# Normalised, padded frames kept in DRAM: written once in the statistics pass, read again by the 5x5 convolution and by the last layer, which multiplies straight out of PSUM

## The chip, the cores and the metric

The kernel runs on one core of one Trainium2 chip. The metric is the device time of one launch in microseconds (us): the median of the runs shown.

## The reference, cut to what matters

The input x is 16 images of 32 channels of 128x128, in float32. Four layers follow, each of the form x + f(gn(x)), where gn normalises groups of two channels. Layer 0 is a recurrent (LSTM) sweep over diagonals. Layer 1 is an adder layer: minus the sum of |patch - w| over 3x3 taps and 32 channels, on quantised values. Layer 2 mixes 32x32 modes of a Hartley transform. Layer 3, which the change touches, is this:

```
orig = x                                  # here x is gn(x3), x3 the result of layer 2
y = conv3x3(get_operator(x), conv1)       # five normalised edge operators, then a 3x3 conv
y = maxpool2(y); y = conv3x3(y, conv2); ... ; y = deconv2x2(y, deconv3)
y = conv3x3(y, conv7)
return orig * y                           # and the layer returns x3 + orig * y
```

So the result is x3 + gn(x3) * y. The edge operators and the first 3x3 convolution are folded into one 5x5 convolution, whose weights depend on means and variances of the operators' outputs over each image.

## The kernel before

**Stages.** `stage0` does layer 0. `rest` does everything else. In it, `Differences.run` does layer 1: for each of 16 images and 2 halves it makes 72 difference tiles of 128 x 8192 float16 values, some on VectorE (line 708), the others on ScalarE (line 705), and TensorE sums each (line 595). Which engine makes the next one is decided while the program is written, by whichever is planned to be done first.

**Layers 2 and 3 are background work.** `After.work` is a Python generator that handles images in four groups of four. Group g can start when image 4g + 3 has left layer 1. Its steps are `forward` (transform), `encoder` and `last`. `encoder` runs `back` (the inverse transform, which writes x3 to DRAM), `first_layers` (`statistics`, the weight tables, `conv1`, conv2) and `small_layers`. A partition holds one channel of one of the group's four images.

**The order is written out by a planner.** `Weave` holds planned clocks for TensorE, VectorE and ScalarE (`weave.pe`, `weave.dve`, `weave.act`). A background step that yields a positive number takes so many planned us of TensorE; a negative one is a pause; `later(us, step)` puts a step off; `("done", v)` has a put-off step carried out and waits for its planned end. Background TensorE work is put between the sums of layer 1 as long as the sums are not planned to be more than 3 us late (`SLACK`). `keep_busy` (line 625) fills holes in TensorE with matmuls by zero weights. `keep_order` then fixes each engine's queue in just this order; all large DMAs are on SyncE's queue (SP) and are issued in that order too, each behind the waits of those before it. Groups 0 to 2 are woven into layer 1. When layer 1 is done, `drain` alternates between what is left of them (the "left" chain) and group 3 (the "right" chain).

**Frames.** `frames` (line 1283 on) holds a ring of tiles `xp` of [128, 20, 132]: 16 rows of x3, two more above and below, and a border of two columns. The left chain has two such tiles, the right four. `load` (line 1307) brings half a tile from x3, rows of 512 bytes; `normalise` (lines 1309 to 1323) scales and shifts it on ScalarE (1313), zeroes the outermost row on GpSimd (1316), and copies the reflected row (1317) and columns (1319, 1320). This is done for all 16 halves in `statistics` (Gram matmuls at line 1354, edge columns at 1384), and once more for all 16 in `conv1` (matmuls at line 1671). A half is reloaded 2 us of plan after its last use.

**The last layer.** `last` (line 1735 on) loads x3 in four units of 32 rows into `xr` (line 1742), computes the composed deconv3 and conv7 into PSUM (lines 852 and 877), and for each of 8 rounds and 4 images does two VectorE instructions of 128x512:

```
s = acc * istd + (istd * bias + 1)        # line 1800, TENSOR_SCALAR, written interleaved
x = (x - mean) * s                        # line 1763, SCALAR_TENSOR_TENSOR
```

`done` then adds the mean on ScalarE (line 1773), and `store` writes a unit to the output in four DMAs of 4 KB rows (line 1779).

Of the kernel before, what the change touches and what calls it, by code (L numbers as in the profile page):

```python
# [16 lines left out]
HW = H * W  # L17
CHW = C * HW
NG = 4
M1 = 32  # L20
RND = 12582912.0


# [882 lines left out]
class After:  # L906
# [379 lines left out]
    def frames(self, g, pool):  # L1286

        nc, x3, weave = self.nc, self.d["x3"], self.weave
        ring = [pool.tile([128, 20, W + 4], F32, name=f"xp{i}") for i in range(self.buffers["frames"])]
        for t in ring:
            nc.vector.memset(t[:, :, 0], 0.0)
            nc.vector.memset(t[:, :, W + 3], 0.0)

        chunk = lambda ch: ring[ch % len(ring)]

        def parts(ch, half):

            lo, hi = max(16 * ch - 2 + 10 * half, 0), min(16 * ch + 8 + 10 * half, H)
            off = lo - (16 * ch - 2)
            return chunk(ch), lo, hi, chunk(ch)[:, off : off + hi - lo, 2 : W + 2]

        def load(ch, half):
            t, lo, hi, v = parts(ch, half)
            nc.sync.dma_start(v, bc_view(x3, g).rearrange("p (h w) -> p h w", w=W)[:, lo:hi, :])

        def normalise(ch, half, us):
            t, lo, hi, v = parts(ch, half)  # L1310

            def step():
                nc.scalar.activation(v, v, AF.Identity, bias=self.shift3, scale=self.stats3[:, 1])  # L1313
                for edge, r, src, zero in ((lo == 0, 1, 3, 0), (hi == H, 18, 16, 19)):
                    if edge:
                        nc.gpsimd.memset(t[:, zero, :], 0.0)
                        nc.scalar.copy(t[:, r, 2 : W + 2], t[:, src, 2 : W + 2])
                own = slice(10 * half, 10 * half + 10)
                nc.scalar.copy(t[:, own, 1], t[:, own, 3])  # L1319
                nc.scalar.copy(t[:, own, W + 2], t[:, own, W])  # L1320
                weave.act += 2.0

            return weave.later(us, step)

        return load, normalise, chunk

    def statistics(self, g, pool, frames, sides, out, tables):

# [4 lines left out]


        nc, cst, weave = self.nc, self.cst, self.weave
        load, normalise, chunk = frames
# [26 lines left out]
        for ch in range(H // 16):  # L1363
            xp = chunk(ch)
            yield ("done", ready[ch, 0])
            for l in range(2, 18):
                if l == 8:
                    yield ("done", ready[ch, 1])
                r = 16 * ch + l - 2
                own = [r2 for r2 in (r, r + 1) if (r, r2) in GRAM_AT]  # L1370
                if own:
# [21 lines left out]
                weave.dve += 0.3  # L1393

                def following(ch=ch, half=half):
                    load((ch + ahead) % 8, half)
                    if ch + ahead < H // 16:
                        ready[ch + ahead, half] = normalise(ch + ahead, half, 18.0)

                ready[ch + ahead, half] = weave.later(2.0, following)  # L1400
            yield -1.0
# [210 lines left out]
    def conv1(self, g, pool, frames, y1, sides, wf, b1):  # L1612
# [9 lines left out]
        load, normalise, chunk = frames  # L1622
        ahead = self.buffers["frames"]
        ready = {(n // 2, n % 2): normalise(n // 2, n % 2, 4.0 + 3.0 * n) for n in range(2 * ahead)}
        p = self.acc()
        for j in range(4):
            nc.tensor.matmul(p[32 * j : 32 * j + 32, :4], tap_of("all", 25), cst["m4_bc"], start=True, stop=True)
# [30 lines left out]
        spreads = []  # L1658
        for ch in range(H // R):
            xp = chunk(ch)  # L1660
            yield ("done", ready[ch, 0])
            yield ("done", ready[ch, 1])

            acc = [self.acc() for _ in range(4)]
            edge = {0: ("t", 0, 0, 1), H // R - 1: ("b", 3, 3 * W, 17)}.get(ch)
# [32 lines left out]
            yield SUMMED  # L1698
            if ch + ahead < H // R:
                for half in range(2):  # L1700
                    load(ch + ahead, half)
                    ready[ch + ahead, half] = normalise(ch + ahead, half, 26.0 + 4.0 * half)
            out = []
            for blk in range(4):
                a4 = acc[blk].rearrange("p (r w) -> p r w", w=W)
# [21 lines left out]
    def last(self, g):  # L1727

        nc, tc, cst, weave = self.nc, self.tc, self.cst, self.weave
        with self.pool("l_y") as yp, self.pool("l_x", self.buffers["l_x"]) as xp:  # L1730
# [1 line left out]
            y6 = self.y6  # L1732
            up = self.up7.loaded(yp)

            def at(t, unit, j):
                first = t.offset + g * 4 * CHW + (32 * unit + 8 * j) * W
                return bass.AP(t.tensor, first, [[HW, 32], [CHW, 4], [1, 8 * W]])

            def load(unit):
                xr = xp.tile([128, 4, 8 * W], F32, name="xr3")  # L1740
                for j in range(4):
                    nc.sync.dma_start(xr[32 * j : 32 * j + 32], at(self.d["x3"], unit, j))
                return xr

            xr = [load(unit) for unit in range(ahead)]

# [7 lines left out]
            nc.vector.tensor_copy(ms, p[:, :8])  # L1754
            mean, istd = ms[:, 0:4], ms[:, 4:8]

            one = yp.tile([128, 4], F32, name="l_one")
            nc.vector.tensor_scalar(one, istd, up.bias, 1.0, ALU.mult, ALU.add)
            yield -4.0

            def multiply(x, s, pr, blk):
                v = x[:, blk].rearrange("p (r a w) -> p a r w", a=2, w=W)[:, pr]
                nc.vector.scalar_tensor_tensor(
                    v, v, mean[:, blk : blk + 1], s.rearrange("p r w b -> p r (w b)"), ALU.subtract, ALU.mult
                )
                weave.dve += 0.7


            following = {}

            def done(x, unit):
                for blk in range(4):
                    nc.scalar.activation(x[:, blk], x[:, blk], AF.Identity, bias=mean[:, blk : blk + 1])
# [16 lines left out]
            for unit in range(4):  # L1790
                complete(unit - ahead)
                x = xr[unit]
                for pr in range(2):
# [2 lines left out]
                        yield from up.round(y6, 64, acc, lambda j: (2 * pr + pc, 16 * unit + 4 * j, 4, 256 * pc))  # L1796
                    yield SUMMED
                    for blk in range(4):
                        s = yp.tile([128, 4, 64, 2], F32, name="s", bufs=3)
                        nc.vector.tensor_scalar(  # L1800
                            s.rearrange("p r w b -> p b r w"),
                            acc[blk].rearrange("p (b r w) -> p b r w", b=2, w=64),
                            istd[:, blk : blk + 1],
                            one[:, blk : blk + 1],
                            ALU.mult,
                            ALU.add,
                        )
# [134 lines left out]
def program(nc, tc, a, at, out):  # L1942
    def scratch(name, *shape):
        return nc.dram_tensor(name, shape, F32, kind="Internal").ap()
# [4 lines left out]
    d["y6"] = scratch("y6_d", NG, 128, 66 * 66)  # L1949
# [30 lines left out]
```

## Time and profile before

| what | value |
|---|---|
| median of 3 runs | 7199.5 us (7186.45 to 7207.52) |
| span of the profiled execution, first to last instruction | 7206.6 us |
| layer 0 | 0 to about 880 us |
| layer 1 with the background work of groups 0, 1 and a part of 2 | about 880 to 5942 us |
| what is left after layer 1 | 5942 to 7206.6 us |
| `conv1` of groups 0 and 1 | 2824 to 3330 us, 4450 to 4970 us |
| `last` of groups 0 and 1 | about 3530 to 3700 us, 5190 to 5355 us |
| group 2 at 5942 us | in `statistics`: about a quarter of its matmuls done |

No total is recorded for the profiled execution besides its span, which is 7.1 us above the median and inside the interval of the runs.

In the profile's rows, a line is a line of the kernel; "x" is a count; "busy" is the sum of durations; a row of the windows view gives, for a stretch of time, each engine's busy time with the number of its instructions, the TensorE clock granted as a share of full speed, the share of time for which the 16 DMA engines were busy, and GB/s. Rows of a timeline give start, duration, engine, line, operation, tiles and count; the idle time ahead of it and what ended it stand in brackets. Consecutive instructions of one engine overlap a little, so the distance of two starts, not the duration, is what an instruction takes from the engine.

### The profile page before, as it was taken

How to read it: one execution, taken by the hardware profiler on the slowest of the kernel's cores; microseconds unless marked ns; L12 is line 12 of the kernel's file. 1: busy time of each engine (PE TensorE's matmuls, PEld its weight loads, DVE VectorE, ACT ScalarE, POOL GpSimd, SP SyncE). 2: the span in 40 equal slices, each digit the busy share in tenths (PEclk: the TensorE clock that was granted, in tenths of full speed). 3: DMA queues.
4: the chain of work that ended last, by engine and by line, in shares of the span. 5: the costliest groups of instructions: out<-in, count | busy, mean ns of one | idle time of the engine just before them, and what ended most of it. 6: DMA issues, size and time to landing. Idle time of an engine off the chain costs nothing. (4 is left out here: it accounts for less than half of the span.)

```text
span 7206.6 us, 271424 instructions
## 1 busy us (share of the span) xinstructions
PE 5631.0 (78%) x127740; PEld 3001.3 (42%) x127740; DVE 5845.3 (81%) x7099; ACT 5498.0 (76%) x3100; POOL 111.8 (2%) x91
## 2 busy tenths in 40 slices
PE   4778567777877777998777787999776784797896
PEld 3665333333334343333334343333333443554564
DVE  7787689999998989999998999999998994134224
ACT  2555489999998989999999999999998991131222
POOL 0000000000000000000000001000000000000000
PEclk9899789999988898999888998999888986798997
DMA  8664211111133432221343343221252245252324
GB/s 310 230 205 144 83 63 57 55 58 47 47 101 93 141 98 81 63 69 47 78 126 98 115 118 104 65 65 46 57 134 92 64 136 150 89 170 74 86 51 98
DMA packets 372719, 722.57 MB, mean 100 GB/s; under 512 B 50896, under 2 KB 217296, under 8 KB 360720
## 3 DMA queue, kind: packets, MB, share of 16 engines
q1 hardware_dynamic: 364128, 670.79, 30.6%
q0 software_dynamic: 7040, 33.80, 1.4%
q8 instruction: 999, 16.37, 1.0%
q14 instruction: 120, 0.98, 0.0%
q10 hardware_dynamic: 432, 0.64, 0.0%
HBM read 507.28 MB, written 164.32 MB: 93 GB/s over the span
## 5 line engine op out<-in xcount | busy, mean ns | idle before, releaser
L705 ACT ACTIVATE d_act<-q,neg 128x8192 f16<-128x8192 f16 (+1 forms) x631 | 4462.6, 7143 | 184.4 <-PE acc L595 135.0
L708 DVE TENSOR_SCALAR d_dve<-q,qw 128x8192 f16<-128x8192 f16 (+1 forms) x1673 | 3859.4, 2362 | 200.8 <-PE acc L595 158.0
L595 PE MATMUL acc<-d_dve,sel 128*32 128x512 f16 x26768 | 1869.8, 402 | 504.0 <-DVE d_dve L708 454.0
L595 PEld LDWEIGHTS <-sel 128*32 128x32 f16 x36864 | 1026.9, 100 | 2164.4 <-issue 1507.8
L1671 PE MATMUL acc<-xp,wf 32*32 32x512 f32 x25600 | 1043.7, 618 | 37.6 <-issue 32.8
L595 PE MATMUL acc<-d_act,sel 128*32 128x512 f16 x10096 | 724.4, 408 | 356.2 <-ACT d_act L705 343.6
L1671 PEld LDWEIGHTS acc<-xp,wf 32*32 32x32 f32 x25600 | 431.9, 104 | 416.5 <-issue 329.6
L625 PE MATMUL acc<-q,zero 128*32 128x512 f16 x7248 | 522.9, 401 | 0.0
L1609 ACT ACTIVATE y<-pooled,b 32x128 f32<-32x128 f32 x488 | 195.0, 400 | 414.4 <-DVE pooled L1595 407.8
L207 PE MATMUL pg<-h,wb 64*64 64x20 f32 (+15 forms) x4096 | 395.7, 320 | 106.1 <-DVE h L256 64.8
L852 PE MATMUL acc<-y,u_conv 32*32 32x256 f32 (+1 forms) x9728 | 359.8, 459 | 76.0 <-issue 46.6
L244 ACT ACTIVATE gt<-pg,bias 128x20 f32<-128x20 f32 (+15 forms) x1024 | 315.8, 374 | 80.2 <-PE pg L207 73.1
L1313 ACT ACTIVATE xp<-xp,shift,stats 128x1280 f32<-128x1280 f32 (+1 forms) x128 | 182.6, 1434 | 240.5 <-DMA xp<-x_d 210.1
L207 PE MATMUL pg<-e,wb 64*64 64x20 f32 (+15 forms) x4096 | 353.1, 315 | 16.4 <-DVE e L260 5.4
L207 PEld LDWEIGHTS pg<-h,wb 64*64 64x64 f32 x4096 | 248.3, 154 | 140.7 <-DVE h L256 90.4
L625 PEld LDWEIGHTS <-zero 128*32 128x32 f16 x7248 | 218.6, 102 | 203.0 <-issue 46.1
L207 PE MATMUL pg<-xn,wb 64*64 64x28 f32 (+61 forms) x4096 | 284.5, 302 | 11.3 <-ACT gt L244 3.8
L207 PEld LDWEIGHTS pg<-e,wb 64*64 64x64 f32 x4096 | 251.5, 156 | 92.1 <-DVE e L260 62.9
L1354 PE MATMUL acc<-xp 32*64 32x204 f32 (+3 forms) x8576 | 238.5, 344 | 37.8 <-ACT xp L1319 28.8
L1800 DVE TENSOR_SCALAR s<-acc,l_ms,l_one 128x512 f32<-128x512 f32 x128 | 102.3, 824 | 199.0 <-PE acc L852 199.0
L255 ACT ACTIVATE th<-c 128x20 f32<-128x20 f32 (+15 forms) x256 | 81.3, 320 | 235.5 <-DVE c L253 234.1
L852 PEld LDWEIGHTS acc<-y,u_conv 32*32 32x32 f32 x9728 | 171.4, 110 | 196.6 <-issue 130.4
(215 smaller groups left out, 4303.1 us busy)
## 6 DMA issues: line engine op xcount, KB each, us to landing
xr<-x_d SPq DMA_DIRECT2D x192, 512.0 KB
xp<-x_d SPq DMA_DIRECT2D x112, 640.0 KB
q<-q_d SPq DMA_DIRECT2D x32, 2145.0 KB
x_d<-xr SPq DMA_DIRECT2D x128, 512.0 KB
x_in<-in_x_dram SPq DMA_DIRECT2D x16, 2048.0 KB
res<-in_x_dram SPq DMA_DIRECT2D x64, 512.0 KB
xn<-in_xs_dram SPq DMA_DIRECT2D x64, 512.0 KB
xn<-xn SPq DMA_DIRECT2D x128, 256.0 KB
```

The lines of the kernel that those rows point to most:

```text
L207: nc.tensor.matmul(bank[c][q][64 * pair : 64 * pair + 64, :, :width], wb[half, 4 * kind + KIND[q]].rearrange("p b o -> p (b o)"), v[half], ...
L244: nc.scalar.activation(gt[:, q, :, :n], bank[c][q][:, :, :n], AF.Tanh if q == G else AF.Sigmoid, bias=bias[:, KIND[q] : KIND[q] + 1],)
L595: self.nc.tensor.matmul(acc[k][32 * j : 32 * j + 32, :], self.sel16[:, i // 9, :], d[:, row : row + 4, c : c + W], start=first, stop=last,)
L625: self.nc.tensor.matmul(acc[k][32 * j : 32 * j + 32, :], self.zero, q[:, :4, :W], start=False, stop=False)
L705: nc.scalar.activation(dst, src, AF.Relu, bias=self.neg[:, i : i + 1])
L708: nc.vector.tensor_scalar(dst, src, self.qw[:, i : i + 1], 0.0, ALU.subtract, ALU.max)
L852: nc.tensor.matmul(acc[blk][32 * j : 32 * j + 32, o : o + rows * n], t[part, 4 * par + tap, :], src[part, top : top + rows, left : left + ...
L1313: nc.scalar.activation(v, v, AF.Identity, bias=self.shift3, scale=self.stats3[:, 1])
L1354: nc.tensor.matmul(gram[blk][j : j + width, at : at + n], xp[part, l, 2 + j : 2 + j + width], xp[part, rows, j : j + width + 4], start=sta ...
L1609: nc.scalar.activation(d, s, AF.Identity, bias=bj)
L1671: nc.tensor.matmul(acc[blk][32 * j : 32 * j + 32, :], tap_of("all", tap)[rows], xp[rows, 4 * j + kh : 4 * j + kh + 4, kw : kw + W], start= ...
L1800: nc.vector.tensor_scalar(s.rearrange("p r w b -> p b r w"), acc[blk].rearrange("p (b r w) -> p b r w", b=2, w=64), istd[:, blk : blk + 1] ...
```

## The change

1. A DRAM tensor `xn` holds every padded, normalised frame: 128 x 132 x 132 values for each group. (An unused tensor, `y6`, goes.)
2. In `statistics`, each half of a frame is stored to `xn` as soon as it is normalised, so 16 DMAs more for each group. A half whose next content is for `conv1` is not loaded from x3 but read back from `xn` (`again`), border included.
3. `conv1` reads its other halves from `xn` too and neither normalises nor waits for a normalising step. The GpSimd memset of the zero row becomes a VectorE memset.
4. `last` loads its units from `xn` (rows of 132, so 4224 bytes for 8 rows), and one SCALAR_TENSOR_TENSOR takes the place of the two VectorE instructions: x = (acc + (1/istd + bias)) * x, with acc read from PSUM in the interleaved order and x already normalised. It is planned at 0.75 us where the two were planned at 0.65 and 0.7.
5. The output of a unit is stored in 16 DMAs of 512-byte rows, since the rows in `xr` are now 132 apart.

The diff, cut to its core:

```diff
@@ frames
-                        nc.gpsimd.memset(t[:, zero, :], 0.0)
+                        nc.vector.memset(t[:, zero, :], 0.0)
...
+        def padded(ch, top, bottom):
+            return self.d["xn"][g].rearrange("p (h w) -> p h w", w=PW)[:, 16 * ch + top : 16 * ch + bottom, :]
+        def store(ch, half):
+            top, bottom = (0 if ch == 0 else 2, 10)[half], (10, 20 if ch == H // 16 - 1 else 18)[half]
+            nc.sync.dma_start(padded(ch, top, bottom), chunk(ch)[:, top:bottom, :])
+        def again(ch, half):
+            own = slice(10 * half, 10 * half + 10)
+            nc.sync.dma_start(chunk(ch)[:, own, :], padded(ch, own.start, own.stop))
@@ statistics
             yield ("done", ready[ch, 0])
+            store(ch, 0)
             for l in range(2, 18):
                 if l == 8:
                     yield ("done", ready[ch, 1])
+                    store(ch, 1)
...
-                    load((ch + ahead) % 8, half)
                     if ch + ahead < H // 16:
+                        load(ch + ahead, half)
                         ready[ch + ahead, half] = normalise(ch + ahead, half, 18.0)
+                    else:
+                        again(ch + ahead - H // 16, half)
@@ conv1
-        ready = {(n // 2, n % 2): normalise(n // 2, n % 2, 4.0 + 3.0 * n) for n in range(2 * ahead)}
...
-            yield ("done", ready[ch, 0])
-            yield ("done", ready[ch, 1])
...
-                    load(ch + ahead, half)
-                    ready[ch + ahead, half] = normalise(ch + ahead, half, 26.0 + 4.0 * half)
+                    again(ch + ahead, half)
@@ last
-                xr = xp.tile([128, 4, 8 * W], F32, name="xr3")
+                xr = xp.tile([128, 4, 8 * PW], F32, name="xr3")
...
-            nc.vector.tensor_scalar(one, istd, up.bias, 1.0, ALU.mult, ALU.add)
+            nc.vector.reciprocal(one, istd)
+            nc.vector.tensor_scalar(one, one, up.bias, None, ALU.add)
...
-                for j in range(4):
-                    nc.sync.dma_start(at(self.out, unit, j), x[32 * j : 32 * j + 32])
+                for blk in range(4):
+                    for j in range(4):
+                        first = self.out.offset + (g * 4 + blk) * CHW + (32 * unit + 8 * j) * W
+                        rows = bass.AP(self.out.tensor, first, [[HW, 32], [W, 8], [1, W]])
+                        nc.sync.dma_start(rows, inner(x)[32 * j : 32 * j + 32, blk])
...
-                        s = yp.tile([128, 4, 64, 2], F32, name="s", bufs=3)
-                        nc.vector.tensor_scalar(s..., acc[blk]..., istd[...], one[...], ALU.mult, ALU.add)
-                        weave.dve += 0.65
-                        if blk:
-                            multiply(x, previous, pr, blk - 1)
-                        previous = s
-                    multiply(x, previous, pr, 3)
+                        v = inner(x)[:, blk, pr::2].rearrange("p r (w b) -> p r w b", b=2)
+                        nc.vector.scalar_tensor_tensor(
+                            v, acc[blk].rearrange("p (b r w) -> p r w b", b=2, w=64),
+                            one[:, blk : blk + 1], v, ALU.add, ALU.mult)
+                        weave.dve += 0.75
```

More of the change, by code (lines that the diff above doesn't have):

```diff
@@ L20 @@
 M1 = 32
+PW = W + 4
+PADDED = PW * PW
 RND = 12582912.0
@@ L1323, in normalise @@
             return weave.later(us, step)
-        return load, normalise, chunk
+        def padded(ch, top, bottom):
[6 more added lines that the diff above has]
+            nc.sync.dma_start(chunk(ch)[:, own, :], padded(ch, own.start, own.stop))
+        return load, normalise, store, again, chunk
     def statistics(self, g, pool, frames, sides, out, tables):
         nc, cst, weave = self.nc, self.cst, self.weave
-        load, normalise, chunk = frames
+        load, normalise, store, again, chunk = frames
         ahead = self.buffers["frames"]
@@ L1620, in tap_of @@
             return wf[:, const if i == size else at + i, :]
-        load, normalise, chunk = frames
+        _, _, _, again, chunk = frames
         ahead = self.buffers["frames"]
-        ready = {(n // 2, n % 2): normalise(n // 2, n % 2, 4.0 + 3.0 * n) for n in range(2 * ahead)}
         p = self.acc()
@@ L1733, in last, with inner @@
             up = self.up7.loaded(yp)
-            def at(t, unit, j):
-                first = t.offset + g * 4 * CHW + (32 * unit + 8 * j) * W
-                return bass.AP(t.tensor, first, [[HW, 32], [CHW, 4], [1, 8 * W]])
             def load(unit):
-                xr = xp.tile([128, 4, 8 * W], F32, name="xr3")
+                xr = xp.tile([128, 4, 8 * PW], F32, name="xr3")
+                t = self.d["xn"]
                 for j in range(4):
-                    nc.sync.dma_start(xr[32 * j : 32 * j + 32], at(self.d["x3"], unit, j))
-                return xr
+                    first = t.offset + g * 128 * PADDED + (2 + 32 * unit + 8 * j) * PW
+                    rows = bass.AP(t.tensor, first, [[PADDED, 32], [32 * PADDED, 4], [1, 8 * PW]])
+                    nc.sync.dma_start(xr[32 * j : 32 * j + 32], rows)
+                return xr
+            def inner(x):
+                return x.rearrange("p b (h w) -> p b h w", w=PW)[:, :, :, 2 : W + 2]
             xr = [load(unit) for unit in range(ahead)]
@@ L1757, in last @@
             one = yp.tile([128, 4], F32, name="l_one")
-            nc.vector.tensor_scalar(one, istd, up.bias, 1.0, ALU.mult, ALU.add)
+            nc.vector.reciprocal(one, istd)
+            nc.vector.tensor_scalar(one, one, up.bias, None, ALU.add)
             yield -4.0
[L1761 to L1766, printed above, removed]
             following = {}
@@ L1772, in done @@
                 for blk in range(4):
-                    nc.scalar.activation(x[:, blk], x[:, blk], AF.Identity, bias=mean[:, blk : blk + 1])
+                    v = inner(x)[:, blk]
+                    nc.scalar.activation(v, v, AF.Identity, bias=mean[:, blk : blk + 1])
                 weave.act += 4.4
@@ L1798, in last @@
                     for blk in range(4):
-                        s = yp.tile([128, 4, 64, 2], F32, name="s", bufs=3)
[L1800 to L1803, printed above, removed]
+                        v = inner(x)[:, blk, pr::2].rearrange("p r (w b) -> p r w b", b=2)
+                        nc.vector.scalar_tensor_tensor(
+                            v,
+                            acc[blk].rearrange("p (b r w) -> p r w b", b=2, w=64),
                             one[:, blk : blk + 1],
+                            v,
+                            ALU.add,
                             ALU.mult,
-                            ALU.add,
                         )
-                        weave.dve += 0.65
-                        if blk:
-                            multiply(x, previous, pr, blk - 1)
-                        previous = s
-                    multiply(x, previous, pr, 3)
+                        weave.dve += 0.75
                     yield -2.5
@@ L1948, in program @@
     d["xm"], d["z"] = (scratch(n, B, C, M1, M1) for n in ("xm_d", "z_d"))
-    d["y6"] = scratch("y6_d", NG, 128, 66 * 66)
+    d["xn"] = scratch("xn_d", NG, 128, PADDED)
     d["fold"] = scratch("fold_d", 5, 128, 90 * 32)
```

## Prediction

> **What bounds the kernel now.** I read the windows view by stage first, since the program is several programs one after the other. The columns are TensorE, its weight loads, VectorE, ScalarE, GpSimd, clock, DMA.
>
> ```profile
> 920.00:5942.00 5022.00, 4055.13 (x85482) 1903.55 (x85489) 4738.98 (x3849) 4799.37 (x1233) 91.48 (x51) 0.92 0.28 83
> 2824.00:3330.00 506.00, 492.03 (x11016) 186.28 (x11008) 478.71 (x315) 494.58 (x215) 1.47 (x1) 0.98 0.18 53
> 5942.00:6075.00 133.00, 69.66 (x1810) 48.66 (x1794) 44.09 (x100) 21.55 (x38) 4.05 (x4) 0.73 0.52 138
> 6200.00:6450.00 250.00, 237.00 (x6834) 139.46 (x6813) 73.69 (x187) 65.46 (x147) 6.00 (x12) 0.96 0.41 124
> ```
>
> While layer 1 runs (first row), VectorE is busy 94% and ScalarE 96% of the time; in `conv1` of group 0 (second row) TensorE is full as well. After 5942 us (last rows) VectorE and ScalarE are a third busy and TensorE, or a wait, sets the pace. So work taken from VectorE or ScalarE counts only before 5942 us. Next, what the change removes, by line, and in the timeline of group 0's `last`:
>
> ```profile
> L1800 DVE TENSOR_SCALAR s<-acc,l_ms,l_one 128x512 f32<-128x512 f32 x128 | 102.3, 824 | 199.0 <-PE acc L852 199.0
> L1763 DVE SCALAR_TENSOR_TENSOR xr<-xr,l_ms,s 128x512 f32<-128x512 f32 x128 | 93.4, 753 | 0.0
> ```
> ```profile
> 3572.07 1.53 DVE L1800 TENSOR_SCALAR s<-acc,l_ms,l_one 128x512 f32<-128x512 f32 x2
> ...
> 3577.59 4.64 DVE L708 TENSOR_SCALAR d_dve<-q,qw 128x8320 f16<-128x8320 f16 x2
> ```
>
> Durations overlap: four pairs take 3577.59 - 3572.07 = 5.52 us, so a pair takes 1.38 us of VectorE, not 0.82 + 0.75. The same for a normalising step, on ScalarE:
>
> ```profile
> 3043.69 1.46 ACT L1313 ACTIVATE xp<-xp,shift,stats 128x1280 f32<-128x1280 f32 x1
> 3045.19 0.21 ACT L1319 COPY xp<-xp 128x10 f32<-128x10 f32 x1
> 3045.30 0.21 ACT L1320 COPY xp<-xp 128x10 f32<-128x10 f32 x1
> 3045.41 1.47 ACT L1313 ACTIVATE xp<-xp,shift,stats 128x1280 f32<-128x1280 f32 x1
> ```
>
> One step takes 3045.41 - 3043.69 = 1.72 us. Last, the waits view of SP's queue: SP already stands for long at its head, which matters for stores put into it.
>
> ```profile
> SPq L1307 <- PE acc L1354: 307.6, 51, 33.0
> SPq L1307 <- DVE sides L1384: 150.4, 26, 12.7
> ```
>
> **What the skill says.** The Trainium skill, Vector Engine (DVE) Microarchitecture Reference, section Measured stream behaviour on trn2, measures SBUF streams: full rate (1.054 ns per column) only for runs of two adjacent words, 1.73 ns when one source hops at every element. The new instruction reads PSUM with a hop of 1 KB at every element. No row of before reads so; for a hopping output the trace agrees, since the copy of line 1230 takes 1051 ns where line 1241's contiguous instruction takes 688. DMA: Bandwidth & Descriptors, section Two DMAs through the same engine are not ordered, says that the issuing engine must wait for the first DMA's completion before it issues a dependent one. So a reload of a frame half must stand at SP's head until the store that reads that half has finished. No run here shows that wait yet.
>
> **The change part by part**, against the profiled span of 7206.6 us.
>
> *VectorE in `last`.* Groups 0 and 1 run it inside layer 1 (64 of the 128 pairs). The new instruction is bounded by line 1763's distance of starts, 3574.17 - 3573.51 = 0.66 us, and by line 1230's kind, 1051 ns less the same overlap of 0.08, so 0.97 us. I take 0.85: the hop alternates between only two runs. It saves 64 x (1.38 - 0.85) = 33.9 us (26.2 to 46.1). Freed time goes to layer 1's tiles, which both engines share. A tile takes 2.28 us of VectorE (five from 3560.69 to 3572.07) or 7.03 of ScalarE (3014.89 to 3021.92), so the pair makes 0.439 + 0.142 = 0.581 tiles a us, and a VectorE us is worth 0.439/0.581 = 0.755 us of time, a ScalarE us 0.245. Hence 33.9 x 0.755 = 25.6 us (19.8 to 34.8).
>
> *ScalarE in `conv1`.* Groups 0 and 1 lose 2 x 16 steps, 32 x 1.72 = 55.0 us, worth 55.0 x 0.245 = 13.5 us. The zero row's memset on VectorE is one instruction of at most 0.27 us (line 153's 258 wide) for four edges, under 1 us; taken at nothing, since the two removed waits behind GpSimd's are as small. Layer 1 ends 25.6 + 13.5 = 39 us earlier (33 to 48).
>
> *What is given back.* The background loses those 39 us too. Group 2's `statistics` makes 2144 matmuls there in some 178 us (line 1354, group 0: 2542 to 2720), 12 a us, so 470 more of them remain at the end of layer 1. Afterwards they go at 1656 in 133 us, 12.5 a us: 38 us. So the left chain is ahead by only 39 - 38 = 1 us, the right one (group 3) by 39. They share TensorE, which is 95% busy from 6200 to 6580 us, so the end moves by something between; I take the mean of 1 and 39, 20, and add 3 because `forward` of group 3 fills a TensorE that is half idle until 6200 us. That is 16 given back (0 to 38).
>
> *Stores to `xn`.* 16 in each group. In layer 1 SP issues them: 0.36 us each (line 1307's median), with 48 more output DMAs for each group, 64 x 0.36 to 0.53 = 23 to 34 us of a queue with 5022 us. Behind a store that waits for ScalarE stand loads of layer 1's next image (xq, q), issued 10 tiles or more, some 17 us, ahead: hidden, and if that cover is gone each late one costs ScalarE its wait. After 5942 us the left chain has two frames only, and its DMAs are saturated (0.52 of the window, full from 5975 to 6000 us): 5 us lost (0 to 20).
>
> *Reads from `xn`.* Rows of 5280 bytes instead of ten of 512. TensorE's idle gaps in group 3's `conv1` of some 4.5 us (at 6706, 6799, 6852 us) coincide with bursts of frame loads, with no wait that the profile shows. Shorter bursts should save about one such gap in each late `conv1` and one shared: 5 us (0 to 12). Queue order is as before; a frame is read back one (left) or three (right) chunks ahead, 24 to 45 us, against 7.8 us from issue (6832.35) to use (6840.13).
>
> *The tail.* After the last matmul VectorE does 4 x 0.85 instead of 5.5 us: 2 saved. The last unit goes out in 16 DMAs of 512-byte rows instead of 4; the first four need only the first image, so they leave earlier, while 12 more issues at 0.36 take 4.3 us: 1 lost (0 to 6). Elsewhere after 5942 us the removed ScalarE and VectorE work lies beside TensorE: nothing. If TensorE were to stall there, VectorE's 64 x 0.53 us would show at most.
>
> Sum: 39 - 16 - 5 + 5 + 2 - 1 = 24 us. 7206.6 - 24 = 7182.6; the span stands 7.1 us above the median, so **7175.5 us** on the median's scale.
>
> **The rivals.** *(A) Nothing is given back*: TensorE's holes take the extra matmuls. For it: 80 us idle in 6075 to 6200. Against: `conv1` must wait for them. 7175.5 - 16 = 7159.5. *(B) TensorE keeps all*: the left chain's 1 us decides, 1 - 5 + 5 + 2 - 1 = 2 us gained: 7197.5. For it, 95% in the windows above. The case that the change doesn't do what it says, a new instruction as slow as the pair, lands near here too: 13.5 us of ScalarE, of which as large a share is given back. *(C) Slower: reloads behind stores.* In `statistics` with two frames, each of 12 reloads waits at SP for the store of that half. A half's matmuls take about 8 us of the 133/8 = 16.6 for a chunk, and a transfer of this size landed 7.8 us after issue; if traffic makes it 14, each reload is 6 us later, on the left chain after 5942 us, and 12 x 6 - 24 = 48 us are lost: 7247.5. From 24/12 = 2 us for each reload the gain is gone; from (24 + 21.6)/12 = 3.8 it is slower by over 0.3%. Against it: loads now stand at SP for PE anyway, up to 33 us.
>
> **How the numbers follow.** Likeliest case 40%, A 20%, B 22%, C 18%. A measurement can tell about 0.3%, 21.6 us, from no change, so faster means below 7177.9, slower above 7221.1. The likeliest case spans 7150 to 7200 and lies two thirds below 7177.9, since its middle does (27%); A all of it (20%), B a tenth (2%): 49% faster. C ends slower in 16 of its 18, and 4% of the others do with full end bounds: 20%. Same: 31%. The range leaves out the lower fringe of A and of C what lies beyond (24 + 28.5)/12 = 4.4 us for each reload: 7138 to 7228.
>
> **What would show it.** Right: the single SCALAR_TENSOR_TENSOR at 0.74 to 1.05 us; 64 rows of line 1313's kind, not 128; layer 1's last tile near 5900 us; group 2's Gram matmuls nearly all after it. Given-back time shows as group 2's `conv1` starting near 6200. C shows in SP's waits as frame loads behind DMAs that read xp, and as ScalarE waiting for xp. Wrong: layer 1 not ending at least 25 us earlier, or VectorE waiting longer for PE in it.

## The result and the profile after

| | before | after |
|---|---|---|
| median of 6 runs each | 7197.43 us (7186.45 to 7207.52) | 7177.82 us (7169.13 to 7185.48) |
| ratio | 1 | 0.9971, 95% interval 0.9958 to 0.9983 |
| span of the profiled execution | 7206.6 us | 7183.6 us |
| layer 1's tiles, first to last | 919.6 to 5941.5 us | 917.3 to 5908.2 us |
| from there to the end | 1265.1 us | 1275.4 us |

The changed kernel is faster by 0.29%, some 21 us, about the least that a measurement can tell from no change. It wins 33 us by the end of layer 1 and gives 10 of them back afterwards. The forecast was 7175.5 us. The time is right; below it turns out that errors of some 20 us in it cancelled.

The windows view of the kernel after, by stage (stretch, length, then busy time and count of TensorE, its weight loads, VectorE, ScalarE, GpSimd; clock, DMA share, GB/s):

```profile
920.00:5910.00 4990.00, 4000.13 (x84910) 1884.09 (x84902) 4678.34 (x3748) 4752.38 (x1114) 63.20 (x38) 0.92 0.28 86
5910.00:6040.00 130.00, 74.68 (x1383) 47.54 (x1380) 49.80 (x137) 17.07 (x31) 6.19 (x8) 0.67 0.66 206
6200.00:6450.00 250.00, 229.29 (x6521) 133.27 (x6532) 69.02 (x190) 50.05 (x114) 5.79 (x11) 0.93 0.47 159
```

Layer 1 (first row) is 31 us shorter from its first tile to its last, and VectorE and ScalarE are still the full engines in it: 94% and 95%. Right after it (second row) TensorE is busy for 57% of the time at DMAs of 206 GB/s, where it was 52% at 138 before.

The page's row of the normalising steps before, then its rows for what the change made:

```profile
L1313 ACT ACTIVATE xp<-xp,shift,stats 128x1280 f32<-128x1280 f32 (+1 forms) x128 | 182.6, 1434 | 240.5 <-DMA xp<-x_d 210.1
```
```profile
L1315 ACT ACTIVATE xp<-xp,shift,stats 128x1280 f32<-128x1280 f32 (+1 forms) x64 | 91.1, 1433 | 285.6 <-DMA xp<-x_d 249.2
L1817 DVE SCALAR_TENSOR_TENSOR xr<-acc,l_one,xr 128x512 f32<-128x512 f32 x128 | 87.2, 744 | 210.2 <-PE acc L854 159.6
```

There are 64 normalising steps instead of 128, and one VectorE instruction of 744 ns in place of two of 824 and 753. The last four of these follow one another in the timeline:

```profile
7169.84 2.73 DVE L1817 SCALAR_TENSOR_TENSOR xr<-acc,l_one,xr 128x512 f32<-128x512 f32 x4 [8.63 <-PE acc L854]
7170.63 4.29 ACT L1787 ACTIVATE xr<-xr,l_ms 128x1024 f32<-128x1024 f32 x4 [16.62 <-DVE xr L1817]
```

Four take 2.73 us, and with 0.744 for the last one that is (2.73 - 0.74)/3 = 0.66 us from start to start, where a pair took 1.38.

What the prediction had no term for stands in the waits view of VectorE in layer 1 (waiting instruction, what it waited for: us in total, times, longest us). The kernel before, then the kernel after, with rows left out at the dots:

```profile
DVE d_dve L708 <- PE acc L595: 158.0, 100, 17.8
DVE xw L1126 <- DMA xw<-xm_d: 43.8, 7, 11.5
...
DVE xh L1019 <- DMA xh<-x_d: 4.2, 2, 4.0
```
```profile
DVE d_dve L710 <- PE acc L597: 153.9, 95, 20.2
...
DVE wf L1502 <- DMA v<-fold_d: 25.9, 4, 12.3
DVE xw L1128 <- DMA xw<-xm_d: 25.0, 5, 6.6
DVE xh L1021 <- DMA xh<-x_d: 22.0, 2, 17.8
```

The waits for `wf` are new, and those for `xh` five times as long; those for `xw` fell from 44 to 25 us. `wf` builds group 1's weight table and `xh` is a load of group 1's transform: both sit on VectorE ahead of layer 1's tiles, and both wait for DMAs that are queued on SP.

### The profile page after: what moved, and what is told of

Same layout as the page of the kernel before. It is cut to its first block, busy times and chain, and to the rows that moved or that the text cites. A ratio compares the mean times of both kernels' runs of the same rounds, so it can differ in the third digit from the quotient of the medians.

```text
span 7183.6 us, 271275 instructions
## 1 busy us (share of the span) xinstructions
PE 5609.0 (78%) x127660; PEld 2987.4 (42%) x127660; DVE 5742.7 (80%) x6972; ACT 5412.1 (75%) x2911; POOL 84.5 (1%) x75
## 5 line engine op out<-in xcount | busy, mean ns | idle before, releaser
L1688 PEld LDWEIGHTS acc<-xp,wf 32*32 32x32 f32 x25600 | 410.1, 104 | 409.9 <-issue 318.7
L854 PE MATMUL acc<-y,u_conv 32*32 32x256 f32 (+1 forms) x9728 | 343.4, 446 | 56.9 <-issue 46.6
L1370 PE MATMUL acc<-xp 32*64 32x204 f32 (+3 forms) x8576 | 255.5, 359 | 67.4 <-ACT xp L1321 55.2
L1315 ACT ACTIVATE xp<-xp,shift,stats 128x1280 f32<-128x1280 f32 (+1 forms) x64 | 91.1, 1433 | 285.6 <-DMA xp<-x_d 249.2
L1370 PEld LDWEIGHTS acc<-xp 32*64 32x64 f32 (+1 forms) x8576 | 181.1, 141 | 180.0 <-issue 115.1
L1817 DVE SCALAR_TENSOR_TENSOR xr<-acc,l_one,xr 128x512 f32<-128x512 f32 x128 | 87.2, 744 | 210.2 <-PE acc L854 159.6
```

The lines of the kernel that those rows point to most:

```text
L854: nc.tensor.matmul(acc[blk][32 * j : 32 * j + 32, o : o + rows * n], t[part, 4 * par + tap, :], src[part, top : top + rows, left : left + ...
L1370: nc.tensor.matmul(gram[blk][j : j + width, at : at + n], xp[part, l, 2 + j : 2 + j + width], xp[part, rows, j : j + width + 4], start=sta ...
L1688: nc.tensor.matmul(acc[blk][32 * j : 32 * j + 32, :], tap_of("all", tap)[rows], xp[rows, 4 * j + kh : 4 * j + kh + 4, kw : kw + W], start= ...
L1817: nc.vector.scalar_tensor_tensor(v, acc[blk].rearrange("p (b r w) -> p r w b", b=2, w=64), one[:, blk : blk + 1], v, ALU.add, ALU.mult,)
```

## An account of layer 1 that all runs share

I split layer 1, from its first tile's start to its last tile's end, in every trace: the waits are the sum over the waits view of an engine; "other work" is the time, from start to start and without waits, of all instructions that are not difference tiles. "Rest" is from there to the end of the span. Ratios are to the kernel before, with 95% intervals.

| kernel | ratio | layer 1 | VectorE waits / other work | ScalarE waits / other work | rest |
|---|---|---|---|---|---|
| before | 1 | 5021.9 | 292 / 926 | 260 / 349 | 1265.1 |
| after | 0.9971 (0.9958 to 0.9983) | 4990.9 | 319 / 876 | 275 / 283 | 1275.4 |
| conv1's half alone | 1.0091 (1.0075 to 1.0106) | 5045.3 | 337 / 925 | 296 / 282 | 1310.1 |
| last's half alone | 1.0083 (1.0069 to 1.0096) | 5081.9 | 387 / 878 | 338 / 352 | 1263.4 |
| last's half, stores from GpSimd | 1.0066 (1.0053 to 1.0080) | 5086.2 | 393 / 878 | 343 / 351 | 1254.1 |
| after, stores twice | 1.0020 (1.0011 to 1.0028) | 5007.8 | 338 / 876 | 293 / 283 | 1306.2 |
| after, stores from GpSimd | 0.9939 (0.9925 to 0.9952) | 4975.2 | 305 / 876 | 260 / 283 | 1256.0 |
| after, 4 output DMAs | 0.9993 (0.9985 to 1.0001) | 4989.6 | 318 / 876 | 273 / 283 | 1299.9 |
| after, real padding | 0.9904 (0.9890 to 0.9917) | 4934.0 | 217 / 922 | 185 / 290 | 1292.2 |
| after, plan padded only | 0.9919 (0.9907 to 0.9932) | 4937.9 | 269 / 879 | 197 / 290 | 1291.0 |
| after, plan padded elsewhere | 1.0056 (1.0041 to 1.0070) | 5046.5 | 376 / 880 | 317 / 282 | 1285.7 |
| after, plan padded, GpSimd | 0.9901 (0.9885 to 0.9917) | 4944.1 | 275 / 878 | 203 / 290 | 1285.0 |
| before, real padding | 1.0115 (1.0102 to 1.0129) | 5105.3 | 337 / 968 | 334 / 349 | 1264.1 |
| before, plan padded only | 1.0089 (1.0074 to 1.0104) | 5083.7 | 357 / 925 | 315 / 349 | 1258.0 |

The rates of exchange of the prediction carry over: layer 1 minus 0.755 times VectorE's two numbers minus 0.245 times ScalarE's lies between about 3951 and 3958 us in all fourteen rows. For before it is 5021.9 - 0.755 x 1218.2 - 0.245 x 609.6 = 3952.8. So every difference between rows can be read term by term. This is bookkeeping and no test of a cause: in every row the two engines make 2304 tiles between them, at 2.28 and 7.05 us each from start to start, and the sum holds because these two prices stay the same. Why waits come or go it doesn't say. One flaw of the table: its waits take in the one ahead of each engine's first tile (38 to 40 us on VectorE, 44 to 47 on ScalarE; 33 and 39 with real padding in the kernel after), which lies before the stretch and hardly differs between the other rows. A caution on the last column: each row is one execution, and some lie 5 to 15 us off their median; where the text gives a price in us without more, it is from the ratios.

From before to after: other work 50.1 x 0.755 + 66.5 x 0.245 = 54 us less, waits 26.7 x 0.755 + 14.5 x 0.245 = 24 us more (26 without those ahead of the first tiles), together 30 of the measured 31 us. Not all of the 54 us are saved work. ScalarE has 39 normalising steps fewer in layer 1, 71 before and 32 after: 32 of them are `conv1`'s, gone for good, and seven belong to group 2's `statistics`, which now runs after layer 1. The theory put to the test is the prediction's, with the new waits as its open point; the rivals were A (nothing given back), B (TensorE keeps all) and C (stores and reloads), and later, that the order of the queues decides more than the work.

## Experiments

**One half of the change at a time.** Both halves store the frames in `statistics`. In the first, `last` is as before; in the second, `conv1` is.

```diff
 conv1's half: def last(self, g): as in the kernel before
 last's half:
-                    if ch + ahead < H // 16:
-                        load(ch + ahead, half)
+                    load((ch + ahead) % 8, half)
...
 conv1, last's half:
-                    again(ch + ahead, half)
+                    load(ch + ahead, half)
+                    ready[ch + ahead, half] = normalise(ch + ahead, half, 26.0 + 4.0 * half)
```

> One half of the change alone: frames are stored in the statistics pass and conv1 reads them back, but the last layer stays as before (x3 loaded, two VectorE instructions, four output DMAs of a unit). The prediction's terms for this half: layer 1 shorter by 13.5 us (55 us of ScalarE), about 40% of it given back, 5 us lost by stores, 5 gained by reads: 8 us faster than before, ratio 0.999. If nothing is given back (rival A): 13.5 us, 0.998. If TensorE keeps all (rival B): 0 us, 1.000. If stores and reloads cost what rival C says they do (6 us for each of 12 reloads): 60 us slower, 1.008.

> The other half alone: frames are stored in the statistics pass for the last layer only, which multiplies straight from PSUM and writes 16 DMAs of a unit; conv1 loads x3 and normalises as before. With the 0.66 us from start to start that the new instruction shows, 46 us of VectorE are saved, 34.8 us of layer 1. Theory (about 40% given back, stores 5, tail +1): 17 us faster than before, ratio 0.9976. Nothing given back: 31 us, 0.9957. TensorE keeps all: 4 us slower, 1.0005.

Measured: 7278.45 us against 7211.66, 1.0091; and 7271.28 us, 1.0083. Each half alone is 60 to 67 us *slower*, while the whole is 21 us faster: effects that don't add. Neither half lost its saving: ScalarE's other work is 282 us in the first (349 before), VectorE's 878 in the second (926). What came is waits: 44 and 36 us more in the first, 95 and 77 us in the second (VectorE and ScalarE). VectorE's waits in layer 1 of the second, below the tiles' own:

```profile
DVE xw L1128 <- DMA xw<-xm_d: 79.3, 9, 33.8
...
DVE xr L1819 <- DMA out_dram<-xr: 25.6, 1, 25.6
DVE xr L1243 <- DMA xr<-x_d: 22.4, 2, 21.0
```

`xw` and line 1243's `xr` are parts of the transform, which the change doesn't touch. Line 1819 is the last layer's new instruction, which waits once for a DMA of its own output. Of the forecasts only rival C's number fits, in the first run (1.008, inside the interval), but not its place: 23 us are lost in layer 1, and after it reloads and loads stand 22 us for stores to finish, not 60 or more. In the second none fits. That left two suspects: the stores that both halves share, or where the planner now puts each step.

**The stores: twice, and from another queue.** In these two runs and in the one with 4 output DMAs further down, TensorE, VectorE and ScalarE carry out the same instructions in the same order as in the changed kernel (but for two of VectorE's and under 1% of TensorE's, which trade places with near neighbours). So nothing but the DMAs differs, and in the run with 4 DMAs where ScalarE's adding step writes.

```diff
 stores twice:
             nc.sync.dma_start(padded(ch, top, bottom), chunk(ch)[:, top:bottom, :])
+            nc.sync.dma_start(twin, chunk(ch)[:, top:bottom, :])
 stores from GpSimd:
-            nc.sync.dma_start(padded(ch, top, bottom), chunk(ch)[:, top:bottom, :])
+            nc.gpsimd.dma_start(padded(ch, top, bottom), chunk(ch)[:, top:bottom, :])
```

> The changed kernel with each frame store issued twice (the second to a tensor that nobody reads), so that the cost of the stores and of the reloads that wait for them doubles. Theory: 5 us more (stores lie in a hole of TensorE or beside its work), ratio to before 0.998. If the stores are hidden: 0 us, 0.997. If reloads behind stores decide (rival C), 12 reloads wait 2 us longer or more: 24 us, 1.0005 or more.

> The changed kernel with the 64 frame stores issued from GpSimd's queue, which is nearly idle, so that SP no longer stands 163 us for ScalarE ahead of a store, with loads of layer 1 and of the frames behind it. Reloads still wait for the stores on SP. Theory (the stores cost layer 1 time through SP's order): ScalarE's and VectorE's waits for DMAs in layer 1 fall by 20 to 40 us, ratio to before 0.992 to 0.995. Rival (the waits for ScalarE on SP are hidden, only reloads behind stores count, or nothing): 0.997.

Measured: 7223.62 us, 1.0020, so a second set of stores costs (1.0020 - 0.9971) x 7211 = 35 us; and 7163.24 us, 0.9939, so taking the first set off SP's queue gains 23 us. The stores are not hidden. The second set doubles their bytes too, so the 35 us don't tell the queue from the traffic; the 23 us come with the same bytes to move. SP's waits, whole run, in the kernel after and with stores from GpSimd, with rows left out:

```profile
SPq L1334 <- ACT xp L1322: 163.2, 32, 21.7
SPq L1309 <- DMA xn_d<-xp: 92.1, 20, 24.0
SPq L1309 <- PE acc L1370: 59.4, 16, 16.6
...
SPq L1339 <- DMA xn_d<-xp: 19.3, 6, 5.5
```
```profile
SPq L1309 <- PE acc L1370: 146.1, 26, 21.5
...
SPq L1339 <- DMA xn_d<-xp: 16.5, 8, 6.5
...
SPq L1309 <- DMA xn_d<-xp: 8.0, 5, 2.7
```

On SP a store (line 1334) stands 163 us for ScalarE's normalising step, and loads from x3 (line 1309) stand 92 us for stores to finish. The two lie in different places: of the 92 us, 86 are in layer 1, and of the 163 us, 141 come after it. With the stores elsewhere the first is gone and the second nearly so, though each load still has to wait for its store: the store was itself issued late. In part SP then stands at the same loads for the Gram matmuls that still read the frame (line 1370), 146 us instead of 59. The reads of `xn` (line 1339) wait little for stores in either. The run takes both stands away at once, so it doesn't say which of them costs how much. What happens right after layer 1 shows in ScalarE's waits over the 205 us from there, kernel after and GpSimd:

```profile
ACT xp L1315 <- DMA xp<-x_d: 153.0, 11, 40.5
```
```profile
ACT xp L1315 <- DMA xp<-x_d: 77.4, 7, 17.6
ACT xp L1315 <- DVE xh L1021: 39.8, 1, 39.8
ACT xp L1315 <- DVE t L1027: 18.7, 1, 18.7
```

In the second, two waits are put down to VectorE, so the two first rows alone overstate the difference: all idle time ahead of the normalising steps is 171 us in the kernel after and 149 us with GpSimd. Group 2's Gram matmuls end 206 us after layer 1 in the first and 190 us in the second (216 us with the stores twice). In a part of the timeline of the kernel after, with rows left out, ScalarE and SP take turns:

```profile
6002.57 1.46 ACT L1315 ACTIVATE xp<-xp,shift,stats 128x1280 f32<-128x1280 f32 x1 [16.80 <-DMA xp<-x_d]
...
6004.17 0.20 ACT L1322 COPY xp<-xp 128x10 f32<-128x10 f32 x1
6004.40 0.33 SPq L1334 DMA_DIRECT2D xn_d<-xp  x1
...
6008.78 0.38 SPq L1309 DMA_DIRECT2D xp<-x_d  x1
...
6018.09 1.46 ACT L1315 ACTIVATE xp<-xp,shift,stats 128x1280 f32<-128x1280 f32 x1 [13.71 <-DMA xp<-x_d]
```

The reader is to see a loop: ScalarE's step, the store that SP issues the moment the step's last copy is done, the next load behind it, and ScalarE's next step once that load has landed. In layer 1 the GpSimd version has 14 us less of VectorE's waits and 15 of ScalarE's, 14 us of layer 1 by the rates (15.7 measured); the rest of the gain lies after it, where the Gram matmuls end 16 us sooner.

> The last layer's half of the change alone (stores in the statistics pass; the 5x5 layer loads and normalises as before; 1.0083 with stores on SP), with the stores issued by GpSimd. Theory (stores in SP's order make the waits of VectorE for xw, xr and out_dram, 127 us there against 45 before): these fall back to some 50 us, layer 1 from 5082 to about 5010 us, ratio 0.998 to 1.000. Rival (they come from where background steps fell, not from the stores): 20 us as in the whole change, ratio 1.005 to 1.007.

Measured: 7259.22 us, 1.0066, some 12 us better than with stores on SP, which is not told apart from nothing (the intervals overlap), and VectorE's waits for `xw`, `out_dram` and `xr` are 87, 24 and 23 us. Layer 1 is not shorter than with the stores on SP (5086.2 and 5081.9 us). The theory that the stores on SP make these waits falls, and most of the 60 us has another cause.

**The output in 4 DMAs.** ScalarE's adding step writes its rows together, so that a unit leaves as before the change.

```diff
-                    v = inner(x)[:, blk]
-                    nc.scalar.activation(v, v, AF.Identity, bias=mean[:, blk : blk + 1])
+                    v = x[:, blk, : 8 * W].rearrange("p (h w) -> p h w", w=W)
+                    nc.scalar.activation(v, inner(x)[:, blk], AF.Identity, bias=mean[:, blk : blk + 1])
...
+                for j in range(4):
+                    first = self.out.offset + g * 4 * CHW + (32 * unit + 8 * j) * W
+                    rows = bass.AP(self.out.tensor, first, [[HW, 32], [CHW, 4], [1, 8 * W]])
+                    nc.sync.dma_start(rows, x[32 * j : 32 * j + 32, :, : 8 * W])
```

> The changed kernel, but the ScalarE step that adds the mean writes the 128-wide rows together at the tile's start, so that an output unit leaves in 4 DMAs of 4 KB rows as before the change, not in 16 of 512-byte rows. Prediction's term: the 16 DMAs cost 1 us in the tail and nothing in layer 1: ratio 0.997. Rival (192 more issues on SP, 0.36 us each, and four times the packets delay loads of the transform that follows, seen as VectorE waiting 22 us for xh and 10 for out_dram): layer 1 up to 30 us shorter, ratio 0.993 to 0.995.

Measured: 7206.23 us, 0.9993: *slower* than 16 DMAs by 16 us, and the two intervals don't meet. Layer 1 is as long as in the kernel after (4989.6 and 4990.9 us), and so within 2 us are the waits for `xh` (20 and 22 us) and `out_dram` (8.5 and 9.6), so the rival falls as well, by which the 192 more issues delay the loads of the transform. The whole loss is after layer 1. The last four VectorE instructions and the output behind them, in this kernel:

```profile
7190.30 2.73 DVE L1816 SCALAR_TENSOR_TENSOR xr<-acc,l_one,xr 128x512 f32<-128x512 f32 x4 [13.50 <-PE acc L854]
7191.09 4.29 ACT L1787 ACTIVATE xr<-xr,l_ms 128x1024 f32<-128x1024 f32 x4 [20.05 <-DVE xr L1816]
7195.40 4.89 SPq L1795 DMA_DIRECT2D out_dram<-xr  x4
```

Four DMAs start only when all four images have been added to, and their issue takes 4.89 us; the span ends at 7207.3, 17.0 us after the first of these VectorE instructions starts. With 16 it is 7183.6 - 7169.84 = 13.8 us; there the first four can leave after the first image. That is 3 us. The rest has no shown cause: group 3's `conv1` ends 9 us later, and its last layer takes 140 us instead of 129. In these last-layer stretches the granted TensorE clock was 0.70 with 4 DMAs and 0.77 with 16, but TensorE's busy time differs by only 6 us (93.5 and 87.6). The run also changes where ScalarE writes, which was not tested by itself.

**The order of the queues.** The first of these was to measure what 36 us of layer 1 are worth at the end, by 72 short VectorE instructions in it.

```diff
 real padding (plan padded only: without the middle lines; elsewhere: 10, 30, 50):
+                    if b >= 4 and i in (20, 40, 60):
+                        first = q.rearrange("p r w -> p (r w)")[:, :512]
+                        nc.vector.tensor_reduce(self.pad, first, AX.X, ALU.max)
+                        weave.dve += 0.66
                     t = dp.tile([128, R, P], F16, name="d_act" if act else "d_dve", ...)
```

> The changed kernel with 72 more VectorE instructions of some 0.66 us in layer 1's images 4 to 15 (a maximum over 512 values that nobody uses), 47.5 us of VectorE, told to the planner too. It measures what a us of layer 1 is worth at the end. All theories: layer 1 ends 36 us later. Theory of the prediction (40% given back): the end moves by 21 us, ratio to before 1.000. Rival A (nothing is given back, or taken): by 36 us, 1.002. Rival B (TensorE keeps all): by 0 to 3 us, 0.997.

Measured: 7144.42 us, 0.9904. With more work, the kernel is 0.67% *faster*. Its VectorE has 46 us more of other work and 102 us less of waits (217 against 319), ScalarE 90 us less. No theory of mine allowed for that, so I took the parts of the padding apart.

> The changed kernel with the 72 steps of 0.66 us added to the planner's VectorE clock in layer 1 only, without the instructions that made the run with real padding 0.7% faster than the changed kernel. Theory (waits decide: the padding helped by moving the background steps and the DMA issues against layer 1's tiles, not by its work): VectorE's waits in layer 1 stay near 217 us, as with real padding, and its 48 us of work go, so layer 1 is up to 36 us shorter than with real padding and the end 20 to 36 us earlier: ratio to before 0.986 to 0.988. Rival (luck of the phase, with no direction): waits anywhere from 200 to 390 us, ratio 0.985 to 1.010. Rival (the padding's own time is what helps, by giving DMAs time): no better than the changed kernel, 0.997.

> The kernel before with the same 72 VectorE instructions of 0.66 us in layer 1, told to the planner. Theory (waits decide in layer 1, whatever kernel): VectorE's 292 us of waits fall too, by more than the 48 us put in, and the kernel gets faster, ratio 0.992 to 0.998. Rival (the padding cured only waits that the change itself made, such as those behind its stores): nothing to cure here, layer 1 is 36 us longer, the end 21 to 36 us later, ratio 1.003 to 1.005.

Measured: 7151.91 us, 0.9919, without any added instruction, so the planner's clock alone does it, not the padding's time: the last rival falls. The first theory falls too: without the instructions VectorE waits 269 us and not 217, and nothing is gained over real padding. The kernel before with padding: 7293.63 us, 1.0115, 82 us slower where the padding's own work is worth 36. Is there a direction in a slower plan, or does each shift draw a new order?

> The changed kernel with the same 72 steps of 0.66 us in the planner's VectorE clock and no instructions, ten tiles earlier in each half image (at tiles 10, 30 and 50 in place of 20, 40 and 60). Theory with a direction (a slower plan puts less background work ahead of the sums in the queues): waits of VectorE in layer 1 near 270 us again, ratio 0.990 to 0.994. Rival (the place of each background step against the tiles decides, and any shift draws anew): waits anywhere from 220 to 390 us, the ratio anywhere from 0.985 to 1.010; 0.997 or more speaks against the direction.

> The kernel before with those 72 steps of 0.66 us in the planner's VectorE clock, at tiles 20, 40 and 60, and no instructions added: no work differs from the kernel before, only the order. With the instructions it was 1.0115. Theory with a direction (a slower plan is better): 0.990 to 0.996. Rival (any shift draws anew): the real padding cost at most 36 us of 7211 there, so without it 1.0115 - 0.005 = 1.0065, slower than before although nothing was added.

Measured: 7256.77 us, 1.0056, and 7277.24 us, 1.0089. The first differs from the kernel of 0.9919 only in that the same 72 steps of plan come ten tiles earlier, and is 1.4% slower. The second does the same work as the kernel before, to the microsecond (925 of other work on VectorE against 926, 349 on ScalarE), in another order, and is 0.9% slower. A slower plan has no direction of its own. Waits in layer 1, of the changed kernel with the plan padded at tiles 20, 40 and 60:

```profile
DVE d_dve L712 <- PE acc L597: 144.6, 91, 15.3
...
DVE xw L1130 <- DMA xw<-xm_d: 18.9, 5, 7.4
```
```profile
ACT d_act L709 <- PE acc L597: 82.9, 29, 14.7
```

At tiles 10, 30 and 50:

```profile
DVE d_dve L712 <- PE acc L597: 170.1, 97, 33.9
DVE xw L1130 <- DMA xw<-xm_d: 55.2, 7, 30.4
...
DVE xr L1245 <- DMA xr<-x_d: 24.3, 1, 24.3
DVE sides L1404 <- ACT xp L1323: 20.0, 2, 15.6
```
```profile
ACT d_act L709 <- PE acc L597: 179.6, 37, 29.5
```

And of the kernel before, with the plan padded:

```profile
DVE xw L1128 <- DMA xw<-xm_d: 58.2, 7, 32.4
...
DVE xr L1243 <- DMA xr<-x_d: 23.9, 2, 23.5
...
DVE xm L1042 <- DMA xm_d<-xm: 21.0, 1, 21.0
```
```profile
ACT d_act L707 <- PE acc L595: 167.2, 41, 32.3
```

The slow orders have the same marks: a step of the transform on VectorE (`xw`, `xr`, `xm`) that comes to the head of its queue up to 32 us before its DMA has landed, with layer 1's tiles behind it, and ScalarE's tiles that wait longer for TensorE: 97 us more at tiles 10, 30 and 50 than at 20, 40 and 60, and in the kernel before 32 us more with the plan padded than without (167.2 and 135.0). These rows say where the time goes; why a DMA is late in one order and not in another was not followed up. All waits together move by up to 176 us on VectorE and 157 on ScalarE between rows of the table (217 to 393, 185 to 342).

**The two edits that helped, together.**

> The two edits that helped, together: the changed kernel with its frame stores issued by GpSimd (0.9939 alone) and with 72 steps of 0.66 us added to the planner's VectorE clock in layer 1 (0.9919 alone; the changed kernel 0.9971). Theory that they cure different waits: the gains add up, 0.9939 - 0.0052 = 0.989. Rival, that both cure the waits behind the stores: no better than 0.992. Rival, that the second was luck of the phase: 0.99 to 1.00.

Measured: 7143.75 us, 0.9901. It is the fastest median but not distinguishable from the plan alone (0.9919) or real padding (0.9904): whether the gains add is open. It beats the kernels before and after, by 0.99% and 0.70%; given what the plan padded elsewhere did, its plan is a good draw and not a rule.

## Why the prediction was right, and where not

**VectorE in `last`: mechanism right, too small.** I took 0.85 us for the new instruction and 33.9 us saved; it takes 0.66, so 64 x (1.38 - 0.66) = 46 us, at the top of my bounds, or 35 us at the rate of 0.755, and not 25.6. (VectorE's other work is 50 us less in all; the remaining 4 us are not from this instruction.)

**ScalarE in `conv1`: right.** ScalarE has 66.5 us less instead of 55.0, worth 16 and not 13.5 us, but the excess is the seven steps of group 2 that moved behind layer 1. Shared out by steps, `conv1`'s 32 of the 39 come to 54.6 us, as forecast. Together layer 1 lost 54 us of work where I said 39; some 48 of them are saved, the others put off.

**"Hidden": the step that did not hold.** "Behind a store that waits for ScalarE stand loads of layer 1's next image ... hidden", and the removed work's freed time was taken as if the waits of the two engines stayed as they were. They grew by 27 and 15 us, worth 24. The GpSimd run shows about 14 of these as the stores' on SP; that the other 10 or so come with the new order is what is left over, not shown. I had named "VectorE waiting longer for PE" as a sign of error and it didn't come (154 us after, 158 before); what came was VectorE waiting longer for DMAs.

**Stores: mis-sized.** I gave 5 us (0 to 20) for all of them, after layer 1 only. Two runs with an unchanged order of the engines put them at 23 us (what leaving SP's queue gains) and 35 us (what a second set costs), in and after layer 1.

**The tail: wrong sign for the DMAs.** I counted 16 DMAs as 1 us lost; at the end they gain 3 us against 4, and the run with 4 is 16 us slower in all, for the most part without a shown cause. The shorter VectorE end was as said: 2.73 us instead of 5.5, so 2.8 saved where I said 2.

**What is given back: right in its sum, not in its course.** As predicted, group 2's Gram matmuls are all (2144, where 1656 remained before) after layer 1. They end 206 us after it, at 6114 us, 46 us *later* than before, where I had the left chain 1 us ahead: they took 190 us, not 133 + 38. Late frames have their part in that, since with the stores off SP's queue they took 174 us. But group 3's `forward` began 14 us after layer 1's end instead of 64, so that chain was not 39 but 83 us ahead (its statistics end only 43 us ahead, at 6536 instead of 6579). That group 2's remaining work no longer stood before it in the queues is the likely reason, not a tested one. The two met in between as said: 10 us lost after layer 1 for all causes together, where 16 + 5 - 5 - 2 + 1 = 15 was forecast. There is no fixed share that is given back: with layer 1 shorter by 53 and 57 us (plan padded, and real padding, against after) the rest is 16 and 17 us longer; with it 62 and 83 us longer (the same two against before) the rest is 7 and 1 us *shorter*.

**Reads from `xn`, 5 us: not tested by themselves.** In the traces TensorE's idle time ahead of `conv1`'s matmuls after layer 1 falls from 25 to 18 us in group 3 and rises from 10 to 14 in group 2, 4 us less together; with one trace each, and all else changed too, that proves nothing. It stays open, and so does what the first half alone loses after layer 1 (rest 1310 us).

**The rivals.** A and B ask for a rest that is not longer, or as much longer as layer 1 is shorter; it is 10 us longer with 33. C's wait exists, but in another place: in layer 1, where line 1309's loads stand 86 us for stores. After it they stand 5.7 us, and the reads of `xn` 1.6, not 12 x 6. The store that stands for ScalarE, which I had named and called hidden, takes 141 us of SP after layer 1. Both go with the stores, so which of the two costs more stays open.

So the sum came out as 24 us, against 23.0 between the profiled spans, because 15 us more of work gone from layer 1 than forecast, 5 us less lost after it and 2 us by which it began earlier stood against the 24 of waits that the sum lacked. That is luck. And the order that the planner happened to write could as well have given 0.992 or 1.006 for the same work: a result of 0.3% is less than this. In three pairs under the same edit of the plan the change is ahead each time: 0.9971/1, 0.9919/1.0089 = 0.983 and 0.9904/1.0115 = 0.979. But the same edit doesn't give the two kernels the same order, so these are three pairs of draws, and one of the changed kernel's orders (1.0056) is slower than the kernel before. How much the change does of itself, apart from the order, stays open; what it takes off VectorE and ScalarE is sure.

## What to carry to other kernels

In a program whose queues are written out by a planner, price a change in three parts: the work it removes at the full engines' rate of exchange, which can be read off the profile as long as the price of a tile stays the same, as it did here; the DMAs it adds, at the queue's head where they stand, not where they land; and the waits of the full engines, which any shift of the plan draws anew. Measure the last part's spread with a run that changes only the plan (here 1.4%) before believing a result smaller than it. Where a store that waits for an engine stands ahead of that engine's next loads in one queue, try another queue for it: here that was worth 23 us.

## What the runs showed of the hardware that was not expected

- VectorE's instruction of 128x512 that reads PSUM with a hop of 1 KB at every element, between two runs, took 744 ns (line 1817), and the one of the same kind and size that reads PSUM contiguously 743 ns (line 578):

```profile
L578 DVE SCALAR_TENSOR_TENSOR xr<-acc,sumw,xr 128x512 f32<-128x512 f32 x128 | 87.2, 743 | 3.4 <-PE acc L597 3.3
```

  The 1051 ns of line 1230, whose output hops in SBUF and which I used as the upper bound, don't apply to it, and neither does the price for a hopping SBUF source that the prediction cites.
- Many small DMAs were not dearer than few large ones at the end: with 16 of 512-byte rows for the last unit the span ended 13.8 us after the start of the last four VectorE instructions, with 4 of 4 KB rows 17.0 us; the four took 4.89 us to issue.
- GpSimd's queue issued the 64 frame stores at 5.5 to 6.0 us from issue to landing (median) without any cost that shows: VectorE's and ScalarE's other work in layer 1 is the same to 1 us.
